# Layer 0 of a four-layer graph network: 22 strips of whole products, or seven products of half matrices

## The chip, the cores and the metric

The kernel runs on one core of a Trainium2 chip. The metric is the time on the device from the first to the last instruction, in microseconds (us). Before the change the median of three runs is 1968.97 us (1967.04 to 1970.67); the profiled execution has a span of 1967.7 us. "PE" is TensorE, "PEld" its loads of weights (the stationary operand), "DVE" VectorE, "ACT" ScalarE, "POOL" GpSimd and "SP" SyncE, whose queue starts most loads.

## The reference, cut to what matters

There are N = 2708 nodes with F = 256 features, and one weighted adjacency matrix `adj` (float32, entries of 0 or above), used by all four layers. Each layer ends with a residual and a normalisation of rows:

```python
x = layernorm(x + adj @ (x * W0))            # layer 0, W0: one factor per feature
x = layernorm(x + gat(x, adj > 0))           # layer 1: attention with 4 heads, softmax over neighbours
x = layernorm(x + signed_gat_gru(x, adj))    # layer 2: attention and two GRU cells
x = layernorm(x + linear(x, adj @ h / deg))  # layer 3: mean over neighbours
```

Layer 0 is a product of 2708x2708 by 2708x256. Layer 1 needs, for every node, `h = x @ W`, two exponentials of its attention logits (called rise and fall below), and the mask `adj > 0`.

## The kernel before, in words

The nodes are cut into NT = 22 tiles of P = 128 rows; the last has 20. `adj_t` is the matrix laid out in DRAM so that `adj_t[t]` is a strip: the 128 columns of tile t with all neighbours on the partitions, 22 blocks of 128x128 side by side.

Layer 0 (L361 to L468) goes strip by strip. For each tile t it loads a strip of 1.4 MB, and `strip_matmul` (L199) multiplies 22 blocks as weights by `x0[c]`, the 256 features of neighbour tile c as moving operand, all summed in one PSUM accumulator of 128x256. The first three strips go side by side, block after block, as x arrives (L421 to L426). The result has its rows on partitions at once. `layer0_mask` (L367) writes the 0/1 mask of the strip as fp8 for layer 1, which holds it for all nodes. `layer0_scale` (L374) multiplies by W0, `layer0_rest` adds x (L380) and normalises (`moments`, L146 to L151, where GpSimd takes a power, and L157). `layer1_projection` turns the tile (L163, two transposes), copies it out of PSUM (L165), projects it (L338, L351), takes the exponentials (L341, L342, L355) and scales `hs[t]` (L343). This is done for tile t - 1 while the products of tile t run, so only the last tile's end stands open after the last product. `xs[t]`, the normalised rows, stay in SBUF.

Layer 1 (L472 to L725) takes the nodes in pairs of groups of columns and, for each pair of heads, goes over the neighbour tiles c = 0 to 21: DVE makes two tiles p (L668) from fall, rise and mask, PE multiplies them by `hs[c]` (L650) and by columns of ones (L659).

Layers 2 and 3 (L895 on) already use a scheme of seven products. The matrix and the features are cut in two halves each way. The columns are cut in three `units` of 512, 512 and 330 columns in each half (NH = 1354); over MH = 11 pairs of neighbour tiles (c, c + 11), `step` (L977) makes four sums of blocks on DVE (L983 to L986) and seven products of 128x128 by 512 or 330 (L996), in place of eight. The features' own sums, `quarter_sums` (L961), are made once for each pair, on DVE. `sums` (L1000) puts the seven accumulators together. They fill seven of the eight PSUM banks; the eighth, `bank()` (L906), serves all other PE work, one piece at a time. Such pieces are generators, which `between()` (L1178) moves on at given places between the products. A result comes out with features on partitions, so each tile is turned back to rows by two transposes (in layer 3 at L1237).

A tile framework reorders the instructions of each engine by a planner's costs, lets each engine run its own list in order, and puts in the waits: between engines, between a load and its reader, and before a buffer is used again.

Of the kernel before, what the change touches and what calls it, by code (L numbers as in the profile page):

```python
# [27 lines left out]
def kernel(  # L28
# [83 lines left out]
    xs = [xpool.tile([P, F], F32, name=f"x{t}") for t in range(NT)]  # L112

    nc.gpsimd.memset(xs[NT - 1], 0.0)
# [13 lines left out]
    st_d = [dram.tile([2 * K, 2, W], F32, name=f"st_{u}") for u in range(len(units))]  # L128

# [146 lines left out]

    uw = const.tile([P, FC, K], F32, name="uw")
# [34 lines left out]
    if True:  # L312

        w1_a = keep.tile([P, FC, F + 2 * H], F32, name="w1_a")
        nc.scalar.dma_start(w1_a[:, :, H : H + F], w1.rearrange("(c p) j -> p c j", p=P))
# [8 lines left out]
        ps_t = ps_t_stack.enter_context(pool("ps_t", 3, space=PSUM, side="right"))  # L324
        ps_m = m_stack.enter_context(pool("ps_m", 2, space=PSUM, side="right"))
        ps_acc = acc_stack.enter_context(pool("ps_acc", 3, space=PSUM))
        if True:
# [5 lines left out]
            def layer1_projection(pool, t):  # L333
                n = sz(t)
                xt = transposed(ps_t, pool, xs[t], n, "xt")
                pm = ps_m.tile([P, 2 * F], F32, tag="pm", name="pm")
                for f in range(FC):
                    nc.tensor.matmul(  # L338
                        pm[:n, : F + H], xt[:, f, :n], w1_a[:, f, H:], start=(f == 0), stop=(f == FC - 1)
                    )  # L340
                nc.scalar.activation(rise[:n, t, :], pm[:n, F : F + H], AF.Exp, scale=1.0 - ALPHA)  # L341
                nc.scalar.activation(hs[t][:n, :, HD], pm[:n, F : F + H], AF.Exp, scale=ALPHA)  # L342
                nc.vector.tensor_tensor(  # L343
                    hs[t][:n, :, :HD],
                    pm[:n, :F].rearrange("p (h d) -> p h d", d=HD),
                    hs[t][:n, :, HD:].to_broadcast([n, H, HD]),
                    ALU.mult,
                )
                pf = ps_t.tile([P, 4, P], F32, tag="tr", name="pf")
                for f in range(FC):  # L350
                    nc.tensor.matmul(  # L351
                        pf[:, 0, :n], w1_a[:, f, :P], xt[:, f, :n], start=(f == 0), stop=(f == FC - 1)
                    )
                fall = pool.tile([H, P], F32, tag="fall", name="fall")
                nc.scalar.activation(fall[:, :n], pf[:H, 0, :n], AF.Exp, scale=ALPHA - 1.0)  # L355
                nc.gpsimd.dma_start(fall_d[:, t * P : t * P + n], fall[:, :n])

                for g in [g for g, (lo, hi) in enumerate(spans[:4]) if hi == t + 1]:
                    load_fall(falls[g // 2], g, nc.gpsimd)

            with pool("l0", 2) as l0:  # L361
                w0_b = l0.tile([P, F], F32, name="w0_b", bufs=1)
                nc.scalar.dma_start(w0_b, bcast(w0, F))

                def layer0_mask(t, s, lo=0, hi=NT):
                    n = sz(t)
                    nc.vector.tensor_scalar(  # L367
                        mask[:, lo:hi, t * P : t * P + n], s[:, lo:hi, :n], 0.0, None, ALU.is_gt, saturate=False
                    )

                def layer0_scale(t, acc):
                    n = sz(t)

                    nc.vector.tensor_tensor(xs[t][:n], acc[:n, :F], w0_b[:n], ALU.mult)  # L374

                def layer0_rest(t, acc=None):
                    n = sz(t)
                    if acc is not None:
                        layer0_scale(t, acc)
                    nc.vector.tensor_tensor(xs[t][:n], xs[t][:n], x0[t][:n], ALU.add)  # L380
                    layernorm(xs[t], xs[t], n)
                    layer1_projection(l0, t)


                ahead = 3
                with pool("prep", side="right") as prep:
                    a1_b = prep.tile([P, 2 * HD], F32, name="a1_b")
# [12 lines left out]
                    for k in range(K):  # L400
                        wk = weights(prep, f"wk{k}", gat_w[k], nc.scalar)
                        ak = prep.tile([P, F], F32, name=f"ak{k}")
# [6 lines left out]
                    strips = [l0.tile([P, NT, P], F32, tag="strip", name="strip", bufs=2) for _ in range(2)]  # L409
                    strips += [prep.tile([P, NT, P], F32, name=f"strip{t}") for t in range(2, ahead + 1)]  # L410
                    accs = [ps_acc.tile([P, 512], F32, tag="acc", name="acc") for _ in range(ahead)]
                    for c0, c1 in blocks:
                        whole = min(c1, N // P)
                        nc.sync.dma_start(
                            turn[:, c0 * F : whole * F].rearrange("p (c f) -> p c f", f=F),
                            x[c0 * P : whole * P, :].rearrange("(c p) f -> p c f", p=P),
                        )
                        for c in range(whole, c1):
                            nc.sync.dma_start(x0[c][: sz(c)], x[c * P : c * P + sz(c), :])
                        for t in range(ahead):  # L420
                            nc.sync.dma_start(strips[t][:, c0:c1], adj_t[t, :, c0:c1])  # L421
                            for c in range(c0, c1):
                                nc.tensor.matmul(  # L423
                                    accs[t][:, :F], strips[t][:, c], x0[c], start=(c == 0), stop=(c == NT - 1)
                                )
                            layer0_mask(t, strips[t], c0, c1)  # L426
                    nc.sync.dma_start(strips[ahead], adj_t[ahead])
                    for t in range(ahead):
                        layer0_scale(t, accs[t])
                    acc = ps_acc.tile([P, 512], F32, tag="acc", name="acc")  # L430
                    strip_matmul(acc[:, :F], strips[ahead], P, lambda c: x0[c])
                    for t in range(ahead):
                        layer0_rest(t)
                    nw = weights(prep, "nw", neigh_w)
                    lw = weights(prep, "lw", lin_w)
# [3 lines left out]
                    for o in range(FC):  # L439
                        pt = ps_t.tile([P, 4, P], F32, tag="tr", name="pt")  # L440
                        for i in range(FC):
                            nc.tensor.transpose(pt[:, i, :], nw[:, i, o * P : (o + 1) * P], ident)
                        nc.scalar.copy(nwt[:, o, :], pt[:, :FC, :].rearrange("p i q -> p (i q)"))
                    for i in range(FC):
                        pt = ps_m.tile([P, 2 * F], F32, tag="pm", name="pt")
                        for o in range(FC):
                            nc.tensor.matmul(
                                pt[:, :F], nwt[:, o, i * P : (i + 1) * P], lw[:, FC + o, :], start=(o == 0), stop=(o == FC - 1)
                            )
                        nc.scalar.copy(lwn2[:, i], pt[:, :F])  # L450
                    nc.gpsimd.dma_start(lwn_d[:, :, F:], lwn2)
                    layer0_mask(ahead, strips[ahead])

                keepr = mask_stack.enter_context(pool("keepr", side="right"))
                gamma_b = keepr.tile([P, F], F32, name="gamma_b")
                beta_b = keepr.tile([P, F], F32, name="beta_b")
                fallp = fall_stack.enter_context(pool("fallp", 2, side="right"))
                falls = [fallp.tile([P, H, 2 * W], F32, tag="fall_b", name="fall_b") for _ in range(2)]
                nc.sync.dma_start(gamma_b, bcast(gamma, F))
                nc.sync.dma_start(beta_b, bcast(beta, F))  # L460
                for t in range(ahead + 1, NT):
                    s = load_strip(l0, t)
                    last, acc = acc, ps_acc.tile([P, 512], F32, tag="acc", name="acc")
                    strip_matmul(acc[: sz(t), :F], s, sz(t), lambda c: x0[c])
                    layer0_mask(t, s)

                    layer0_rest(t - 1, last)
                layer0_rest(NT - 1, acc)  # L468

            m_stack.close()  # L470
            ps_u = m_stack.enter_context(pool("ps_u", space=PSUM, side="right"))
            l1 = keep_stack.enter_context(pool("l1", 2))  # L472
# [1060 lines left out]
```

## Time and profile before

| stretch of the profiled execution | us |
|---|---|
| start to the first product of layer 0 | 6.2 |
| last product of layer 0 ends | 252.5 |
| first product of layer 1 starts | 261.0 |
| end of layer 1's main loop, about | 528 |
| last product of layer 3 starts | 1940.7 |
| end | 1967.7 |

| row of the page | instructions | mean ns |
|---|---|---|
| layer 0's products, 128x256 (L199) | 836 | 379 |
| layer 0's first products (L423) | 132 | 396 |
| layers 2 and 3, products of 512 columns from p with the sums of x (L996) | 352 | 599 |
| the same of 330 columns | 176 | 443 |
| sum of blocks, 128x512 (L983) | 88 | 689 |
| sum of blocks, 128x330 (L983) | 44 | 506 |

A float32 product is two matmul instructions in the trace, so 22 x 22 products of layer 0 are 968 instructions. The mean time of a matmul runs from its start to its modelled end and overlaps the next; the distance between two starts tells what one costs in a full stream. A line of a group gives line, engine, operation, output from inputs, shapes and count, then busy us and mean ns, then the engine's idle time just before and what ended it. A line in order of time begins with start and length in us.

### The profile page before, as it was taken

Reading aid. Unit: us, or ns where it says so; the run is one execution under the profiler, and the core shown is the slowest. Engines: PE = TensorE matmul, PEld = TensorE weight load, DVE = VectorE, ACT = ScalarE, POOL = GpSimd, SP = SyncE. Lnnn points to the kernel's source line nnn. Section 1 sums busy time; section 2 is a strip of 40 time slices with the busy share of each in tenths; the row PEclk is TensorE's granted clock in tenths of the full one; section 3 lists DMA queues with packets and bytes.
Section 4 is the critical chain, followed back from the end, with each engine's and each line's share of the span. In section 5 each row is a group of like instructions: output and inputs, shape, how many; then the busy total and the mean of one; then the engine's idle time right before and its main releaser. Section 6 shows DMA issues by size and latency. Waiting matters only on the chain.

```text
span 1967.7 us, 21033 instructions
## 1 busy us (share of the span) xinstructions
PE 1895.1 (96%) x7028; PEld 945.7 (48%) x7028; DVE 1454.0 (74%) x2364; ACT 852.0 (43%) x1011; POOL 348.8 (18%) x522
## 2 busy tenths in 40 slices
PE   8999999999999999999999999999999999999995
PEld 7888822222333444445545444444445555554443
DVE  5333378898897689999987888585877758745764
ACT  0100045445603367777855656555655555211000
POOL 0211210013515302111210101020110201311211
PEclk9999999999999999999999999999999999999998
DMA  8343333432200786766475756454554535633752
GB/s 288 121 169 140 139 114 126 152 119 97 69 4 19 211 266 221 245 219 202 126 214 164 215 161 180 114 162 120 149 153 119 130 100 136 168 108 105 199 153 78
DMA packets 398210, 293.96 MB, mean 149 GB/s; under 512 B 105354, under 2 KB 379434, under 8 KB 390244
## 3 DMA queue, kind: packets, MB, share of 16 engines
q1 hardware_dynamic: 381180, 237.86, 41.2%
q0 software_dynamic: 10848, 50.23, 7.5%
q10 hardware_dynamic: 6064, 4.42, 0.7%
q8 instruction: 58, 0.95, 0.2%
q14 instruction: 60, 0.49, 0.1%
HBM read 280.03 MB, written 12.40 MB: 149 GB/s over the span
## 4 chain that ended last, share of the span: by engine, by line
PE 70%; DVE 17%; issue 5%; DMA 3%; POOL 2%; ACT 1%; SPq 1%; ACTq 0%; DVEq 0%; POOLq 0%
PE m L996 31%; PE acc L650 9%; PE acc L199 9%; DVE z L852 8%; PE bank L1056 6%; PE den L659 5%; PE bank L1032 3%; PE bank L1107 2%; DVE p L668 2%; DVE none L848 1%; POOL bn_rs L151 1%; PE acc L423 1%; PE pm L338 1%; DMA p<-in_adj_t_dram 1%; SPq L934 1%
## 5 line engine op out<-in xcount | busy, mean ns | idle before, releaser
L668 DVE SCALAR_TENSOR_TENSOR p<-fall_b,rise,mask 128x1024 f32<-128x1024 f32 (+1 forms) x264 | 298.5, 1152 | 37.1 <-PE den L659 18.6
L1198 ACT ACTIVATE p<-st,e_neg 128x1024 f32<-128x1024 f32 (+1 forms) x198 | 197.5, 1040 | 186.1 <-PE m L996 183.6
L996 PE MATMUL m<-p,xq 128*128 128x512 f32 (+1 forms) x528 | 245.6, 547 | 0.8 <-DVE p L984 0.6
L650 PE MATMUL acc<-p,h 128*64 128x512 f32 (+2 forms) x1056 | 228.4, 561 | 3.2 <-DVE p L668 2.7
L996 PE MATMUL m<-s,xq 128*128 128x512 f32 (+1 forms) x528 | 224.7, 542 | 0.4 <-DVE s L985 0.4
L852 DVE CUSTOM_DVE_ANT_0 z<-e_b,none 128x2708 f32<-128x2708 f32 (+1 forms) x66 | 196.7, 2983 | 0.3 <-DVE e_b L822 0.2
L857 ACT ACTIVATE z<-z,st 128x2708 f32<-128x2708 f32 (+1 forms) x66 | 168.5, 2553 | 64.7 <-DVE st L852 63.1
L199 PE MATMUL acc<-turn,strip 128*128 128x256 f32 (+1 forms) x836 | 187.1, 379 | 0.0
L1201 ACT ACTIVATE p<-p 128x1024 f32<-128x1024 f32 (+1 forms) x198 | 179.5, 943 | 0.3
L996 PE MATMUL m<-p,x 128*128 128x512 f32 (+1 forms) x396 | 169.5, 547 | 2.6 <-DVE p L1202 2.6
L1202 DVE TENSOR_TENSOR p<-p,blk 128x1024 f32<-128x1024 f32 (+1 forms) x132 | 142.6, 1095 | 30.9 <-ACT p L1201 16.3
L199 PEld LDWEIGHTS acc<-turn,strip 128*128 128x128 f32 (+1 forms) x836 | 151.9, 185 | 23.5 <-issue 0.2
L262 PE MATMUL s<-blk,x 128*128 128x512 f32 (+2 forms) x416 | 162.9, 545 | 0.0
L983 DVE TENSOR_TENSOR s<-p 128x512 f32<-128x512 f32 (+1 forms) x132 | 82.8, 628 | 97.9 <-PE m L996 83.8
L996 PEld LDWEIGHTS m<-p,xq 128*128 128x128 f32 x528 | 99.3, 191 | 99.6 <-issue 74.6
L996 PEld LDWEIGHTS m<-s,xq 128*128 128x128 f32 x528 | 98.7, 190 | 93.6 <-issue 70.3
L650 PEld LDWEIGHTS acc<-p,h 128*64 128x64 f32 x1056 | 65.2, 137 | 149.5 <-issue 119.8
L659 PE MATMUL den<-p,h 128*32 128x512 f32 (+2 forms) x1056 | 125.9, 557 | 2.3 <-DVE p L668 2.2
L151 POOL TENSOR_TENSOR bn_rs<-bn_rs,neg_half 128x1 f32<-128x1 f32 (+1 forms) x110 | 79.3, 722 | 242.3 <-DVE bn_rs L150 239.4
L262 PEld LDWEIGHTS s<-blk,x 128*128 128x128 f32 x416 | 77.9, 190 | 74.2 <-issue 62.5
L996 PEld LDWEIGHTS m<-p,x 128*128 128x128 f32 x396 | 74.6, 191 | 76.7 <-issue 59.1
L165 ACT COPY xt<-tr 128x256 f32<-128x256 f32 (+1 forms) x44 | 16.0, 363 | 209.2 <-PE tr L163 203.5
(228 smaller groups left out, 2587.5 us busy)
## 6 DMA issues: line engine op xcount, KB each, us to landing
blk<-in_adj_t_dram SPq DMA_DIRECT2D x172, 256.0 KB, 3.8
turn<-in_adj_dram SPq DMA_DIRECT2D x22, 1354.0 KB, 6.0
strip<-in_adj_t_dram SPq DMA_DIRECT2D x19, 1408.0 KB, 6.4
blk<-in_adj_t_dram SPq DMA_DIRECT2D x88, 192.0 KB, 3.9
turn<-in_adj_t_dram SPq DMA_DIRECT2D x65, 256.0 KB, 4.0
arow<-in_adj_dram POOLq DMA_DIRECT2D x10, 1354.0 KB, 6.7
turn<-in_adj_dram POOLq DMA_DIRECT2D x10, 1354.0 KB, 7.2
blk<-in_adj_t_dram SPq DMA_DIRECT2D x103, 128.0 KB, 2.6
```

The lines of the kernel that those rows point to most:

```text
L199: nc.tensor.matmul(acc, s[:, c, :n], rhs(c), start=(c == 0), stop=(c == NT - 1))
L262: nc.tensor.matmul(acc[f][:, :w], xs[c][:, f * P : (f + 1) * P], s[:, c - c0, :w], start=(c == 0), stop=(c == NT - 1),)
L650: nc.tensor.matmul(acc[s][i * HD : (i + 1) * HD, :ws], hs[c][:, 2 * q + i, :HD], ps[i][:, p0 : p0 + ws], **flags,)
L659: nc.tensor.matmul(den[j : j + CT, :ws], hs[c][:, 2 * q + i, HD + 1 - CT :], ps[i][:, p0 : p0 + ws], **flags,)
L668: nc.vector.scalar_tensor_tensor(p[:, :w], falls[g // 2][:, 2 * q + i, :w], rise[:, c, 2 * q + i : 2 * q + i + 1], mask[:, c, at : at + w] ...
L852: nc.vector.tensor_tensor_reduce(out=z[:n], in0=e_b[:n, k, :], in1=none[:n], scale=-1.0, scalar=HIGHEST, op0=ALU.add, op1=ALU.min, accum_o ...
L857: nc.scalar.activation(z[:n], z[:n], AF.Exp, scale=-1.0, bias=st[:n, t, 0, k : k + 1], accum_out=den[:n])
L996: nc.tensor.matmul(dst[:, :w], lt, rt, start=start, stop=stop)
L1056: nc.tensor.matmul(g[:, :w], lt, rt, start=(q == 0), stop=(q == len(terms) - 1))
L1198: nc.scalar.activation(p[:, :, :w], st_k[:, :, :w], AF.Relu, scale=-1.0, bias=e_neg[:, at, k : k + 1])
L1201: nc.scalar.activation(p[:, :, :w], p[:, :, :w], AF.Exp, scale=-1.0)
L1202: made = nc.vector.tensor_tensor(p[:, :, :w], p[:, :, :w], blk[:, i, :, :w], ALU.mult)
```

## The change

Layer 0 gets the scheme of layers 2 and 3. It goes over the three units of columns; for each of 11 pairs of neighbour tiles it loads four blocks of up to 512 columns with `load_pairs`, writes their mask (two operations), makes the four sums and the seven products. The sums of x are made on GpSimd, anew in each unit. `seven` and `combine` are `step` and `sums` of before, with the buffers handed in; `combine` copies the first accumulator straight into its output.

Results have features on partitions. So `layer0_rows` turns each tile back by transposes, scales, adds x, normalises, and stores the rows in DRAM (`x1_d`); `layer0_turned` and `layer1_projection` do what was done before. These three are pieces between products of the next unit, at three places in each step, through the one free PSUM bank. Those of the last unit come after its last product, with three banks.

The region of `xs` in SBUF serves as two of three buffers for the blocks during layer 0, so the rows are loaded back from DRAM for layer 1's end. Layer 1 goes over its neighbours in the order `by_end`, in which their tiles were finished. The small weights are loaded and prepared after the fourth step has been written down. The purpose is to do layer 0's sum with seven products of half size in place of eight.

The diff, cut to its core (`seven`, `combine`, `by_tiles`, `load_pairs` and `between` are moved up, for all layers):

```diff
-    xs = [xpool.tile([P, F], F32, name=f"x{t}") for t in range(NT)]
+    xall = xpool.tile([P, NT * F], F32, name="xall")
+    xs = [xall[:, t * F : (t + 1) * F] for t in range(NT)]
...
+    x1_d = [dram.tile([sz(t), F], F32, name=f"x1_{t}") for t in range(NT)]
...
+            def layer0_rows(t, src):
+                n = sz(t)
+                pt = bank()
+                for f in range(FC):
+                    nc.tensor.transpose(pt[:n, f * P : (f + 1) * P], src[:, f, :n], ident)
+                r = l0.tile([P, F], F32, tag="row", name="row", bufs=3)
+                nc.vector.tensor_tensor(r[:n], pt[:n, :F], w0_b[:n], ALU.mult)
+                nc.vector.tensor_tensor(r[:n], r[:n], x0[t][:n], ALU.add)
+                layernorm(r, r, n)
+                nc.gpsimd.dma_start(x1_d[t], r[:n])
+                return t, r
...
+                for i in range(len(tiles) + 2):
+                    if i < len(tiles):
+                        got.append(layer0_rows(*tiles[i]))
+                        yield
+                    if i >= 2:
+                        layer1_projection(*turned[i - 2])
+                        yield
+                    if 0 < i <= len(tiles):
+                        turned.append(layer0_turned(*got[i - 1]))
+                        yield
...
-                for t in range(ahead + 1, NT):
-                    s = load_strip(l0, t)
-                    last, acc = acc, ps_acc.tile([P, 512], F32, tag="acc", name="acc")
-                    strip_matmul(acc[: sz(t), :F], s, sz(t), lambda c: x0[c])
-                    layer0_mask(t, s)
-                    layer0_rest(t - 1, last)
-                layer0_rest(NT - 1, acc)
+                for u, (a, w) in enumerate(units):
+                    m = accumulators(ps_a)
+                    for c in range(MH):
+                        if u == 0:
+                            for t in (c, c + MH):
+                                nc.sync.dma_start(x0[t][: sz(t)], x[t * P : t * P + sz(t), :])
+                        i = (u * MH + c) % 3
+                        if i < 2:
+                            pa = xall[:, i * 4 * W : (i + 1) * 4 * W].rearrange("p (m h w) -> p m h w", m=2, h=2)
+                        else:
+                            pa = l0.tile([P, 2, 2, W], F32, tag="p", name="p")
+                        load_pairs(u, c, pa)
+                        for j in range(2):
+                            nc.vector.tensor_scalar(
+                                mask[:, c + j * MH].rearrange("p (h n) -> p h n", h=2)[:, :, a : a + w],
+                                pa[:, j, :, :w], 0.0, None, ALU.is_gt, saturate=False,
+                            )
+                        s = l0.tile([P, 3, W], F32, tag="s", name="s", bufs=2)
+                        tt = l0.tile([P, 4, P], F32, tag="xq", name="xq", bufs=3)
+                        seven(
+                            m, pa, s, x0, quarter_sums(nc.gpsimd, tt, x0, c), c, w, c == 0, c == MH - 1, (1, 3, 5)
+                        )
+                        if u == 0 and c == 3:
+                            small_weights()
+                            later.append(neigh_weights())
+                    y = l0.tile([P, FC, 2, W], F32, tag="y", name="y")
+                    combine(m, w, y)
...
+                    later.append(rows0(u, y))
+                ps0_stack.close()
+                banks = ps_t = ps_t_stack.enter_context(pool("ps_t", 3, space=PSUM, side="right"))
+                while later:
+                    between()
...
+            for t in by_end:
+                nc.sync.dma_start(xs[t][: sz(t)], x1_d[t])
...
-                        for c in range(NT):
+                        for j, c in enumerate(by_end):
```

## The prediction

> **What bounds the kernel now.** I read the page's busy shares and the chain that ended last, then layer 0 and layer 3 in tables of windows, because layer 3 already runs the seven products that layer 0 is to get.
>
> ```profile
> PE 1895.1 (96%) x7028; PEld 945.7 (48%) x7028; DVE 1454.0 (74%) x2364; ACT 852.0 (43%) x1011; POOL 348.8 (18%) x522
> PE 70%; DVE 17%; issue 5%; DMA 3%; POOL 2%; ACT 1%; SPq 1%; ACTq 0%; DVEq 0%; POOLq 0%
> ```
>
> TensorE is busy 96% of the span and makes up 70% of the chain. So work taken off it is worth its time, if nothing else becomes the bound.
>
> ```profile
> 0.00:50.00 50.00, 42.19 (x187) 36.58 (x188) 25.39 (x68) 1.66 (x2) 4.79 (x18) 1.00 0.84 285
> 40.00:252.00 212.00, 212.00 (x1041) 182.74 (x1040) 80.37 (x156) 23.66 (x86) 42.40 (x68) 1.00 0.40 144
> 1824.00:1892.00 68.00, 67.55 (x168) 30.13 (x167) 41.77 (x84) 0.58 (x1) 12.37 (x20) 1.00 0.67 185
> 1892.00:1941.00 49.00, 46.52 (x171) 29.80 (x169) 33.47 (x88) 0.43 (x1) 8.17 (x14) 1.00 0.56 146
> ```
>
> The columns after the length are PE, PEld, DVE, ACT, POOL (busy us and count), clock, DMA share, GB/s. Layer 0 (second line) has PE full and DVE only 38% busy. Layer 3's second unit of columns (third line) keeps PE full too, with DVE at 61%; its narrow third unit (fourth line) already loses 2.5 us of PE with DVE at 68%. That is the first warning.
>
> ```profile
> L996 PE MATMUL m<-p,xq 128*128 128x512 f32 x352 | 182.1, 599 | 0.6 <-DVE p L984 0.4
> L199 PE MATMUL acc<-turn,strip 128*128 128x256 f32 x792 | 177.2, 379 | 0.0
> L983 DVE TENSOR_TENSOR s<-p 128x512 f32<-128x512 f32 x88 | 60.6, 689 | 82.7 <-PE m L996 74.3 <-DMA p<-in_adj_t_dram 8.3
> L367 DVE TENSOR_SCALAR mask<-strip 128x2816 fp8e4<-128x2816 f32 x18 | 29.3, 1627 | 47.7 <-DMA strip<-in_adj_t_dram 47.7
> ```
>
> The means of matmuls overlap, so I take their pitch from starts in the order of time: 40 of 128x256 in 8.81 us, 0.216 us each; two steps' starts in layer 3 are 6.01 us apart at 512 columns (14 matmuls, 0.429 each) and 3.886 at 330.
>
> ```profile
> 252.57 0.41 DVE L374 TENSOR_TENSOR x<-acc,w_b 20x256 f32<-20x256 f32 x1 [1.85 <-PE acc L199]
> 258.10 0.41 DVE L343 TENSOR_TENSOR h<-pm,h 20x256 f32<-20x256 f32 x1 [1.82 <-ACT h L342]
> 260.96 1.97 PE L650 MATMUL acc<-p,h 128*64 128x512 f32 x4 [2.65 <-DVE p L668]
> 241.58 0.82 DVE L380 TENSOR_TENSOR x<-x,turn 128x256 f32<-128x256 f32 x1
> 241.40 0.72 POOL L535 TENSOR_TENSOR x<-x,beta_b 128x256 f32<-128x256 f32 x1 [7.75 <-PE tr L163]
> 1430.99 2.34 POOL L953 TENSOR_TENSOR blk<-blk,offdiag 128x128 f32<-128x128 f32 x1 [10.46 <-DMA blk<-in_adj_t_dram]
> 1433.65 0.41 POOL L953 TENSOR_TENSOR blk<-blk,offdiag 128x128 f32<-128x128 f32 x1 [0.31 <-DMA blk<-in_adj_t_dram]
> ```
>
> Layer 0's last product ends at 252.5 and layer 1's first starts at 260.96: one row tile's end lies between, 8.5 us. The last four lines show GpSimd and VectorE in each other's way: a 256-wide sum that takes 0.41 us at the least took 0.82 beside a GpSimd operation, and a GpSimd operation of 0.41 took 2.34 while VectorE ran sums back to back.
>
> [...]
>
> **The change, part by part.**
> *Products.* Removed: 968 matmuls (132 at L423, 836 at L199) x 0.216 = 209 us. Added: 22 steps of 512 columns x 6.01 = 132.2 and 11 of 330 x 3.886 = 42.7, together 174.9. PE gains 34 us. Turning rows back adds two transposes a tile, 0.22 us a pair in layer 3, x 22 = 4.8. Net 29 us less PE: this is what can be won.
>
> *Start.* Now PE starts at 6.23 and by 50 us has lost 7.8. In the built order VectorE does seven small weight operations ahead of the first mask; the first of these starts at 8.23 now (it waits for a load), so masks begin near 11 and PE's third product near 14.5, with two done (1.7 us). PE also waits for a transpose of a weight whose load is tenth on its queue. Loss 12.8, so +5. Unit 0 then ends at 14.5 + 75 products x 0.858 + 2 for weights = 81.
>
> *VectorE and GpSimd beside the products.* A step of 512 needs two masks of 1024 (from 1.63 us for 2816 and 0.43 for 512: 0.70 each) and four sums of 0.69: 4.2 us; of 330: 1.0 + 4 x 0.50 = 3.0. A row tile needs 0.42 + 0.41 + 0.42 + 0.17 + 0.15 + 0.41 + 0.42 = 2.4 us and a wait for GpSimd's power of some 0.75. GpSimd gets four quarter sums a step, 0.41 each alone: 1.7 us, and a tile's power (0.56) and two DMA issues (0.6 each). Two bounds on their meeting: no cost, [...]. For a wide step with a tile the second gives 5.0 (masks, sums, two row operations) + 3.4 = 8.4 us against PE's 6.0 + 1.9 (transposes 0.44, projection 1.5); for a narrow one 3.8 + 3.4 = 7.2 against 5.8. Unit 1 has 7 tiles, unit 2 has 8 (in about 8 of its steps). Unit 1: 7 x 8.4 + 4 x 6.0 = 83, against PE 66 + 14 = 80. Unit 2: 8 x 7.2 + 3 x 4.7 = 72, against PE 42.7 + 15.5 = 58. All small PE work goes through one PSUM bank, so each waits for the reader of the one before; late readers hold up PE. I take 82 and 74 (2 us for loads queued behind a reload, see next); ends 79 and 60, or 88 and 82.
>
> *Tail.* The last unit leaves seven tiles after its last product, where now it is one. Combining takes 2.4 us (layer 3's end: 1941.3 to 1943.7), the first transposes 0.4. A tile costs VectorE 2.4 us of pitch with the power's wait filled, so 17; the last turn and projection 2.5, then 2.5 to the first product of layer 1: 25. The built order of GpSimd has sums of reloaded rows with beta among the powers: store issue 0.58, landing 2.8 (median of like stores), reload issue 0.5 and landing 2.6, the sum 0.72. That round trip of 7.2 us is shorter than two or three tiles, but the powers of tiles 18 and 20 stand behind such sums and VectorE waits behind the powers: some 2.6 us each, twice. I take 30.5 (25 to 36), against 8.5 now.
>
> *Order of layer 1's neighbours, combining without a copy of its own, x reloaded:* nothing; the same operations in another order, under PE's products of layer 1 (261.8 of 266 us busy). More DMA: 22 reloads of 128 KB, hidden there.
>
> Sum to layer 1's first product: 81 + 82 + 74 + 30.5 = 267.5, now 261. Forecast: +6.5, 1968.97 + 6.5 = 1975.5, say 1976.
>
> **The rivals.**
> *PE stays the bound* (as in layer 3 at 1824 to 1892): units end at 79, 79 and 60 us each, tail 25: 243 to 247, so -14: 1955. For it: VectorE's order is planned, and layer 3 lost only 0.45 us in its wide unit. Against: layer 3 has no masks, no quarter sums on GpSimd after its first unit, fewer row operations, and its narrow unit lost 2.5 us all the same.
> *A draw:* contention costs half, unit 2 takes 68 and the tail 28: 81 + 82 + 68 + 28 = 259, 1967. For it: GpSimd may slip into VectorE's gaps. Against: unit 2 has nearly none.
> *VectorE and GpSimd take turns badly:* units 1 and 2 at 88 and 82, tail 36: 287, 1995. For it: powers of 1.46 us occur in the trace where 0.56 is usual. Against: wide steps have slack.
> *DMA bound in unit 0:* 11.5 MB of matrix, 2.8 of x and some 1.5 of weights at the 288 GB/s that the first slice shows take 55 us, under the 66 of products; 4% at most.
>
> **How the numbers follow.** Forecast 0.48, PE-bound rival 0.24, draw 0.14, bad turns 0.10, DMA 0.04. The range, 1958 to 1992, leaves out the best of the PE-bound cases and the worst of the contention. Faster by over 0.2% (under 1965): the PE-bound cases and a few draws, 0.27. Within: 0.15. Slower: 0.58.
>
> **What would show it.** Right: layer 1's first product near 267; VectorE above 85% busy in unit 2, PE idle behind VectorE's reads of the bank and behind mask and sums; quarter sums of GpSimd well over 0.41 us on the mean; some 28 us and more of nearly idle PE before layer 1. Wrong: PE above 97% in units 1 and 2 (then it is faster), or layer 1 itself longer or shorter by more than 3 us, which no step here foresees.

## The result, and the profile after

The changed kernel takes 1989.94 us (median of four, 1987.03 to 1993.66) against 1969.12 for the kernel before: a ratio of 1.0107, 95% interval 1.0088 to 1.0127. It is slower, as forecast, and by 21 us instead of 7. The measured time lies inside the forecast range.

The page of the changed kernel, busy shares and chain by engine:

```profile
PE 1877.6 (95%) x6566; PEld 859.8 (43%) x6566; DVE 1552.4 (78%) x2537; ACT 850.5 (43%) x1014; POOL 440.0 (22%) x682
PE 61%; DVE 16%; DMA 9%; issue 5%; ACT 4%; POOL 4%; SPq 1%; ACTq 0%; DVEq 0%; POOLq 0%
```

TensorE has 17 us less to do, and its share of the chain fell from 70% to 61%: the products did get cheaper, and other things took their place. Where, a table of windows shows, cut at the ends of the three units and at layer 1's first product (after the length: PE, PEld, DVE, ACT, POOL busy and count, granted clock, DMA share, GB/s):

```profile
0.00:25.00 25.00, 8.90 (x12) 3.60 (x13) 10.75 (x21) 1.66 (x2) 7.88 (x24) 0.81 0.80 219
25.00:89.70 64.70, 64.54 (x156) 29.08 (x156) 52.84 (x80) 1.70 (x4) 34.05 (x46) 1.00 0.83 231
89.70:176.50 86.80, 80.96 (x240) 39.18 (x239) 64.38 (x119) 5.80 (x29) 39.61 (x70) 1.00 0.52 143
176.50:246.00 69.50, 61.34 (x250) 41.16 (x249) 53.58 (x121) 8.84 (x34) 40.85 (x73) 0.98 0.53 143
246.00:279.00 33.00, 18.18 (x89) 12.97 (x87) 21.89 (x57) 9.92 (x32) 20.23 (x36) 0.83 0.28 92
```

Unit 2's last product ends at 246.6 us. Layer 1's first product starts at 278.98 where it started at 260.96. From there to the end it is 1706.2 us, before 1706.7: the whole loss lies in layer 0. Up to layer 1's first product TensorE is busy 233.9 us (before 248.6) and idle 45.1 (before 12.4). Of the idle time 16 us lie in the first 25 us, 14 in units 1 and 2, and 15 in the tail; between 25 and 90 us there is next to none (0.2).

In the start TensorE makes two products from 8.7 us on. Then it waits for the load of a weight that it transposes, and after that for a load of the matrix (waits of the first 26 us):

```profile
PE bank L550 <- DMA nw<-in_L_gnn_neigh_W_dram: 3.8, 1, 3.8
PE m L348 <- DMA xall<-in_adj_t_dram: 3.5, 1, 3.5
```

The third product starts at 20.3 us, and the granted clock is 0.50 until 25.5.

What holds TensorE up in units 1 and 2 (waiting operation, what it waited for, total us, times, longest):

```profile
PE bank L454 <- DVE h L473: 7.3, 7, 3.3
PE bank L464 <- DVE row L444: 2.9, 4, 1.1
PE m L348 <- POOL xq L322: 1.2, 1, 1.2
```

`bank` is the one free PSUM bank: each transpose or projection waits until the reader of the piece before, which stands in VectorE's list, has run. The products themselves hardly wait for VectorE's sums. The longest of these waits, 3.3 us, ended at 225.9 us. From 226.9 to 230.3 the granted clock was 0.50, and four matmuls of L464 took 1.94 us there (1.14 at 104.8 us, at a clock of 1.00); so this long wait was followed by slow matmuls too.

The end of the tail, in order of time:

```profile
275.92 0.18 ACT L472 ACTIVATE fall<-bank 4x20 f32<-4x20 f32 x1 [1.80 <-DMA fall_d<-fall]
276.12 0.41 DVE L473 TENSOR_TENSOR h<-bank,h 20x256 f32<-20x256 f32 x1 [3.61 <-ACT fall L472]
...
276.46 4.85 DVE L816 SCALAR_TENSOR_TENSOR p<-fall_b,rise,mask 128x1024 f32<-128x1024 f32 x4
...
278.98 2.83 PE L798 MATMUL acc<-p,h 128*64 128x512 f32 x6 [5.12 <-DVE p L816]
```

The exponential for `fall` of the last, small tile waits for the store of an earlier one (there are two buffers), VectorE's scaling of h waits for it, and everything else behind that.

### The profile page after: what moved, and what is told of

It is laid out like the page before. It is cut to its first block, busy times and chain, and to the rows that moved or that the text cites. A ratio compares the mean times of both kernels' runs of the same rounds, so it can differ in the third digit from the quotient of the medians.

```text
span 1985.2 us, 20983 instructions
## 1 busy us (share of the span) xinstructions
PE 1877.6 (95%) x6566; PEld 859.8 (43%) x6566; DVE 1552.4 (78%) x2537; ACT 850.5 (43%) x1014; POOL 440.0 (22%) x682
## 4 chain that ended last, share of the span: by engine, by line
PE 61%; DVE 16%; DMA 9%; issue 5%; ACT 4%; POOL 4%; SPq 1%; ACTq 0%; DVEq 0%; POOLq 0%
PE m L348 37%; PE bank L1130 6%; DVE z L1000 6%; PE acc L798 5%; DMA turn<-in_adj_dram 5%; PE bank L1106 3%; PE den L807 3%; PE s L263 2%; ACT turn L745 2%; PE bank L1181 2%; POOL bn_rs L152 2%; ACT turn L747 2%; DVE p L816 1%; DVE none L996 1%; DMA xall<-in_adj_t_dram 1%
## 5 line engine op out<-in xcount | busy, mean ns | idle before, releaser
L348 PE MATMUL m<-s,xq 128*128 128x512 f32 (+1 forms) x660 | 282.2, 543 | 0.4 <-DVE s L337 0.4
L348 PE MATMUL m<-p,xq 128*128 128x512 f32 (+1 forms) x572 | 265.6, 547 | 1.3 <-DVE p L336 0.6
L348 PEld LDWEIGHTS m<-s,xq 128*128 128x128 f32 x660 | 123.0, 191 | 114.1 <-issue 86.2
L348 PE MATMUL m<-p,xall 128*128 128x512 f32 (+1 forms) x396 | 169.7, 547 | 2.5 <-DVE p L1249 2.5
L263 PE MATMUL s<-blk,xall 128*128 128x512 f32 (+2 forms) x416 | 164.2, 549 | 0.0
L263 PEld LDWEIGHTS s<-blk,xall 128*128 128x128 f32 x416 | 78.7, 192 | 74.8 <-issue 63.2
L1078 POOL TENSOR_TENSOR blk<-blk,offdiag 128x128 f32<-128x128 f32 (+3 forms) x50 | 43.1, 861 | 299.2 <-DMA blk<-in_adj_t_dram 264.2
L348 PEld LDWEIGHTS m<-p,xall 128*128 128x128 f32 x396 | 74.8, 191 | 76.5 <-issue 59.5
L745 ACT ACTIVATE turn<-turn 128x2708 f32<-128x2708 f32 (+1 forms) x22 | 54.2, 2462 | 98.4 <-DMA turn<-in_adj_dram 97.7
L338 DVE TENSOR_TENSOR s<-p,s 128x512 f32<-128x512 f32 (+1 forms) x143 | 91.0, 636 | 2.1
```

The lines of the kernel that those rows point to most:

```text
L263: nc.tensor.matmul(acc[f][:, :w], xs[c][:, f * P : (f + 1) * P], s[:, c - c0, :w], start=(c == 0), stop=(c == NT - 1),)
L348: nc.tensor.matmul(dst[:, :w], lt, rt, start=start, stop=stop)
```

## The experiments

My theory after the traces was that the loss is made of the start, the hand-over of the one bank, and the tail. The rivals were that GpSimd's sums of x slow VectorE's operations beside them, that the DMA bounds the first unit, and that VectorE's load as such is the limit. Each run was timed in five rounds beside the kernel before on the same chip.

The table has the ratio to the kernel before, and from the profile the time at which ScalarE starts to copy the first accumulator of each unit (a mark 2 to 5 us ahead of the unit's end), the start of layer 1's first and the end of its last product. With * layer 1 starts ahead of the last tiles. Layer 1's loop is counted to its last product, 643.6 us in the kernel before; at about 528 us only two of its three pairs of groups of columns are done. What a unit "took" or is longer or shorter by is, below, the time from mark to mark. The kernel before took 1969.12, 1970.95, 1973.02 and 1972.25 us beside the changed kernel, e1 to e4, e5 to e8 and e9 to e11, so runs of different groups are compared by the ratio and not by their medians. By the ratio only e2, e7, e8, e10 and e11 are clear of the changed kernel's interval.

| kernel | ratio (95%) | unit 0 | unit 1 | unit 2 | first | last |
|---|---|---|---|---|---|---|
| before | 1 | | | | 261.0 | 643.6 |
| after | 1.0107 (1.0088 to 1.0127) | 84.7 | 171.6 | 243.3 | 279.0 | 661.3 |
| e1 fall buffers | 1.0090 (1.0076 to 1.0104) | 83.5 | 170.5 | 242.7 | 273.9 | 662.4 |
| e2 bank by ScalarE | 1.0056 (1.0041 to 1.0071) | 84.5 | 165.3 | 230.7 | 266.4 | 655.5 |
| e3 weights late | 1.0095 (1.0072 to 1.0117) | 82.2 | 168.2 | 239.9 | 274.1 | 662.9 |
| e4 layer 1 ahead | 1.0068 (1.0046 to 1.0090) | 84.3 | 171.3 | 243.3 | 250.2* | 657.2 |
| e5 beta in layer 0 | 1.0086 (1.0062 to 1.0109) | 82.3 | 171.9 | 243.4 | 276.4 | 667.1 |
| e6 weights in unit 1 | 1.0072 (1.0050 to 1.0095) | 71.3 | 165.7 | 237.9 | 273.1 | 662.1 |
| e7 x sums on VectorE | 1.0053 (1.0034 to 1.0072) | 83.8 | 168.2 | 235.9 | 271.4 | 656.8 |
| e8 all together | 0.9987 (0.9972 to 1.0002) | 72.3 | 160.8 | 230.4 | 240.8* | 644.0 |
| e9 masks on ScalarE | 1.0089 (1.0070 to 1.0108) | 81.2 | 163.0 | 238.3 | 273.5 | 660.7 |
| e10 all, x sums on VectorE | 0.9965 (0.9955 to 0.9975) | 71.0 | 156.8 | 225.9 | 235.2* | 638.4 |
| e11 as e10, masks on ScalarE | 0.9967 (0.9952 to 0.9983) | 72.2 | 160.8 | 231.3 | 238.2* | 642.0 |

### e1: more buffers for fall

```diff
-                fall = l0.tile([H, P], F32, tag="fall", name="fall", bufs=2)
+                fall = l0.tile([H, P], F32, tag="fall", name="fall", bufs=8)
```

> The changed kernel with eight buffers for fall in layer 0 instead of two. In its trace the last tile's exponential for fall waits 1.8 us for the store of an earlier fall, and VectorE's scaling of h then waits 3.6 us. If this wait is a part of the tail's length, layer 1's first product comes 2 to 3.5 us earlier and the kernel takes 1987 (1986 to 1988). If the tail is set by the pitch of VectorE's row work alone, nothing moves (within 1 us).

From the mark of unit 2 to layer 1's first product it is 31.2 us instead of 35.6. The wait is gone, and so are, by the planner's choice, the sums with beta among the tail's powers, so that the 4.4 us are not the wait's alone; VectorE's idle time at the wait was 3.6 us. But the time came out at 1988.71, within the noise of the changed kernel. The gain was given back in layer 1, whose loop took 388.5 us instead of 382.3. The groups of VectorE's tiles p and of GpSimd's sums with beta in this kernel, 284 to 314 us (last: busy us, mean ns, idle before):

```profile
L816 DVE SCALAR_TENSOR_TENSOR p<-fall_b,rise,mask 128x1024 f32<-128x1024 f32 x20 | 32.6, 1700 | 0.0
L683 POOL TENSOR_TENSOR xall<-xall,beta_b 128x256 f32<-128x256 f32 x16 | 26.8, 1711 | 0.0
```

The same stretch of the changed kernel (289 to 319 us), where these sums had mostly run in the tail and the end of unit 2:

```profile
L816 DVE SCALAR_TENSOR_TENSOR p<-fall_b,rise,mask 128x1024 f32<-128x1024 f32 x22 | 27.4, 1281 | 3.1 <-PE den L807 1.8 <-PE acc L798 1.2
```

The planner had put the 22 sums elsewhere, and there each tile p took a third longer. TensorE was busy 26.3 of those 30 us.

### e2: the bank emptied by ScalarE

```diff
+                nc.scalar.copy(r[:n], pt[:n, :F])
-                nc.vector.tensor_tensor(r[:n], pt[:n, :F], w0_b[:n], ALU.mult)
+                nc.vector.tensor_tensor(r[:n], r[:n], w0_b[:n], ALU.mult)
...
+                hp = l0.tile([P, 4 * P], F32, tag="hp", name="hp", bufs=2)
+                nc.scalar.copy(hp[:n, : F + H], pm[:n])
+                nc.scalar.copy(hp[:H, 3 * P : 3 * P + n], pf[:H, :n])
+                pm, pf = hp[:, : F + H], hp[:, 3 * P :]
```

> The changed kernel, with the one free PSUM bank emptied by ScalarE copies (rows, and the projection with its logits) in place of VectorE's reads and the exponentials; VectorE then reads SBUF. Theory: TensorE's idle time in units 1 and 2 (14 us in the two) is mostly the wait for late readers of that bank, which stand in VectorE's full list; ScalarE is under 10% busy there, so about 8 us come back: 1982 (1979 to 1985), units 1 and 2 at about 82 and 66 us. Rival, [...]: no change in the units' lengths, or slightly longer [...]: 1990 (1988 to 1993).

The kernel took 1981.25 us. Unit 1 took 80.8 us (86.9 before the edit) and unit 2 65.4 (71.8). That is the expected size, and the "no change" of the rival, GpSimd's sums of x as the cause, is out. (Unit 2's granted clock is 1.00 here and was 0.98, which by estimate, 2% of 71.8 us, is worth some 1.5 us.) TensorE's waits in the two units:

```profile
PE bank L455 <- DVE bn_mv L149: 3.2, 2, 1.7
PE bank L455 <- DVE row L158: 2.3, 2, 1.8
```

The waits for readers of the bank are gone; what is left are transposes that wait for the normalised row itself. Layer 1's loop again took 389.2 us, with the sums with beta in its first 40 us: 6.9 us of the 12.6 won were given back.

### e3 and e6: when the weights come

```diff
-                        if u == 0 and c == 3:
+                        if u == 0 and c == 4:
...
+                        nc.scalar.copy(wk[:, 0, :1], s[:, 0, :1])
                         nc.scalar.dma_start(wk, gat_w[k].rearrange("(c p) j -> p c j", p=P))
```

Each weight's buffer gets such a write from a sum of that step first, so that its load can't come earlier.

> The changed kernel, with the loads of the small weights of layers 1 to 3 (and their work on VectorE and TensorE) held back until the fifth step of layer 0's first unit has made its first sum. Theory: the first unit ended 8.7 us later than forecast because masks and sums stand behind small weight work that waits for loads on a crowded set of queues; without it the first unit ends 5 to 8 us earlier and the kernel takes 1984 (1981 to 1987). Rival, that the matrix's own loads bound the start (219 GB/s in the first 25 us): the first unit ends at most 2 us earlier: 1989 (1987 to 1991).

> The changed kernel with layer 1's small weights held back to the seventh step of the first unit, and those of layers 2 and 3 to the third step of the second, where the DMA share is 0.52 and not 0.9. With all of them held back to the fifth step of the first unit the start was full from 12 us on, but then VectorE stood in front of weights that were late at a DMA share of 0.97 to 0.99, and TensorE idle for 6 us. Theory: the small loads and the matrix together are more than the DMA engines can bring in that unit, and without them the unit ends 6 to 8 us earlier than in the changed kernel (accumulator copied at 77 to 79 us instead of 84.7): 1984 (1981 to 1987). Rival: the matrix and x alone bound the first unit, which ends at 82 or later: 1989 (1987 to 1991).

In e3 (all weights at step 5) the first unit won 2.5 us only, and the time, 1990.04 us, is the rival's. Windows of e3:

```profile
0.00:25.00 25.00, 18.30 (x33) 7.58 (x34) 16.34 (x23) 1.28 (x1) 15.89 (x34) 1.00 0.91 255
25.00:46.00 21.00, 21.00 (x50) 9.12 (x48) 16.86 (x34) 1.51 (x12) 7.81 (x12) 1.00 0.87 227
46.00:55.00 9.00, 3.79 (x8) 1.56 (x8) 6.61 (x10) 0.28 (x2) 3.37 (x5) 0.84 0.94 278
```

The start was as wanted (18.3 us busy in 25 instead of 8.9), then the weights' loads came at a DMA share of 0.94, VectorE stood before a weight that was not there, and the sums of the next step behind it. In e6 layer 1's weights come at step 7 of the first unit (`c == 6`), the others at step 3 of the second:

```profile
0.00:25.00 25.00, 17.43 (x35) 7.01 (x36) 15.98 (x23) 1.28 (x1) 13.93 (x33) 1.00 0.88 248
25.00:73.80 48.80, 48.80 (x115) 21.58 (x114) 41.04 (x60) 0.87 (x3) 24.43 (x35) 1.00 0.79 221
```

From 25 us on TensorE has no gap, and the mark comes 13.4 us earlier, at 71.3. So matrix and x alone do not bound the unit from there on, as the rival had it; matrix, x and weights in the same 60 us, with VectorE's list held at each late weight, do. Unit 1 then carries the weights and takes 94.4 us instead of 86.9, so 5.9 us are left at its end. The forecast of the unit's end was beaten, that of the time missed: the kernel took 1988.49 us (1.0072). Layer 1's loop took 389.0 us; 4.3 of that is one wait of TensorE for ScalarE's copy of a finished accumulator, 1.1 in the changed kernel. e5 (6.3 us) and e3 (4.1) have the same wait.

### e4: layer 1 ahead of the tail

```diff
-                while later:
-                    between()
...
                             for part in (heads, totals)[:: 1 if j % 2 == 0 else -1]:
                                 part(c, ps, dict(start=(j == 0), stop=(j == NT - 1)))
+                            if g == 0 and q == 0:
+                                for _ in range(2):
+                                    between()
```

> The changed kernel, with layer 1's first round over neighbours begun before the last unit's seven tiles are finished: their pieces stand between the products of the fifteen neighbours that are done, with the tail's buffers in the region of x that is free by then, so that no pool has to be closed first. Theory: the tail of 32.5 us, in which TensorE is busy 18 us, some of it at a low clock, is the largest term of the loss, and 10 to 18 us of it come back: 1975 (1972 to 1980). Rival: VectorE, 88% busy in layer 1, has no room for the tail's 22 us, and becomes the bound of that first round: 1987 (1984 to 1992).

This kernel took 1986.06 us. It leaves out the degrees of two row tiles, a little work of layer 1, so its time is if anything too good. From the mark of unit 2 to layer 1's last product it is 414.0 us instead of 418.0: 4 us, not 10 to 18. Layer 1's first product starts at 250.2, but then TensorE waits 6.8 us for tiles p and 2.7 for rows up to 360 us, with VectorE 89% busy from 250 to 290. The sums with beta stand in the same stretch again (1.06 us each, tiles p at 1.37). The rival was nearer.

### e5: beta added in layer 0

```diff
+                rb = l0.tile([P, F], F32, tag="rb", name="rb", bufs=2)
+                nc.gpsimd.tensor_tensor(rb[:n], r[:n], beta_b[:n], ALU.add)
-                nc.gpsimd.dma_start(x1_d[t], r[:n])
+                nc.gpsimd.dma_start(x1_d[t], rb[:n])
...
-                    nc.gpsimd.tensor_tensor(xs[t][:n], xs[t][:n], beta_b[:n], ALU.add)
```

> The kernel with eight fall buffers, and in addition beta added on GpSimd to each row tile before it is stored (so in layer 0's units and tail), in place of the 22 sums with beta on GpSimd after the rows have been loaded back. With eight buffers alone layer 1 began 5 us earlier, but GpSimd's 22 sums stood back to back in layer 1's first 40 us (1.7 us each), VectorE's tiles p took 1.75 us instead of 1.28, and TensorE was busy 8.8 us in 10. Theory: that is what gave the gain back, and with the sums moved into layer 0, where VectorE has about a fifth of its time free, layer 1's first 40 us are full again: 1984 (1981 to 1986.5). Rival: the sums cost the same wherever they stand, and units 1 and 2 get longer by 4 to 5 us: 1988 (1986.5 to 1990).

The kernel took 1989.03 us (1.0086, e1 1.0090): no gain. The mechanism was right, the sum was not. TensorE's 30 us in layer 1 are full (30.00 busy, 26.31 in e1), and its first 352 matmul records there took 62.7 us, not 69.4. But unit 1 and the tail were 2.6 and 1.8 us longer than in e1, and the wait for ScalarE's copy (6.3 us) came on top.

### e7 and e9: VectorE's load, or its turns with GpSimd

```diff
-                            m, pa, s, x0, quarter_sums(nc.gpsimd, tt, x0, c), c, w, c == 0, c == MH - 1, (1, 3, 5)
+                            m, pa, s, x0, quarter_sums(nc.vector, tt, x0, c), c, w, c == 0, c == MH - 1, (1, 3, 5)
```

> The changed kernel with the sums of x (four of 128x128 a step) on VectorE instead of GpSimd. Theory: [...] VectorE then has 1 us more to do in each of 33 steps and reads the bank later: slower by 2 to 10 us, 1995. Rival: [...] then the masks and sums get back to 0.69 us and the powers to 0.56, and units 1 and 2 together get shorter by more than 4 us: 1984.

The kernel took 1982.85 us. My theory, that late readers of the bank hold up units 1 and 2 and GpSimd's sums of x do not, had the wrong sign; the rival, that these sums do, had the right one. Units 1 and 2 got 2.5 and 4.1 us shorter (some 1.5 us of it by the clock in unit 2, an estimate as in e2). Masks and sums went back to 0.69 us, as the rival said; GpSimd's powers did not (0.705 us, before 0.627). The two units of e7, up to the end of their products:

```profile
86.20:170.60 84.40, 80.22 (x240) 39.31 (x239) 68.80 (x165) 5.80 (x29) 15.63 (x24) 1.00 0.53 149
170.60:238.20 67.60, 62.58 (x255) 40.47 (x254) 55.46 (x158) 8.74 (x34) 25.56 (x39) 1.00 0.58 154
```

VectorE, layer 0 in the changed kernel (25 to 246 us):

```profile
L335 DVE TENSOR_TENSOR s<-xall 128x512 f32<-128x512 f32 x14 | 10.8, 770 | 8.3 <-PE m L348 8.1
...
L445 DVE TENSOR_TENSOR row<-row,turn 128x256 f32<-128x256 f32 x15 | 8.7, 577 | 0.1
L158 DVE TENSOR_SCALAR row<-row,bn_mv,bn_rs 128x256 f32<-128x256 f32 x15 | 7.7, 512 | 7.3 <-POOL bn_rs L152 7.3
```

and in e7 (25 to 240 us), with one of the four sums of x:

```profile
L335 DVE TENSOR_TENSOR s<-xall 128x512 f32<-128x512 f32 x14 | 9.6, 686 | 0.2 <-PE m L348 0.2
L319 DVE TENSOR_TENSOR xq<-turn 128x128 f32<-128x128 f32 x31 | 8.8, 284 | 4.2 <-PE m L348 4.2
L445 DVE TENSOR_TENSOR row<-row,turn 128x256 f32<-128x256 f32 x15 | 6.2, 416 | 0.0
L158 DVE TENSOR_SCALAR row<-row,bn_mv,bn_rs 128x256 f32<-128x256 f32 x15 | 6.2, 413 | 7.1 <-POOL bn_rs L152 7.0
```

A sum of x takes VectorE 0.28 us, GpSimd 0.54 to 0.73. In the two windows VectorE was given 81 sums of x, 23.3 us, and was busy only 6.3 us more (124.3 for 118.0): GpSimd's "free" help had cost it some 17 us. (The expectation of e10 has 119.7 for 124.3, from windows that did not reach to the units' ends.)

For e9 the mask is written by `nc.scalar.activation(..., AF.Sign)` instead of `nc.vector.tensor_scalar(..., ALU.is_gt)`, the same for a matrix without negative entries, as this one is.

> The changed kernel with layer 0's masks written by ScalarE as the sign of an entry (the same for a matrix without negative entries, as this one is) instead of VectorE. It takes 1.0 to 1.4 us a step from VectorE, some 40 us in the three units, and nothing else. If VectorE's load (its own work and its turns with GpSimd) is what makes readers late in units 1 and 2, these get shorter by 6 to 12 us together and the kernel takes 1981 (1977 to 1985). If the single bank is held up by latency alone (semaphores, the order of reads), they get shorter by less than 3 us: 1988 (1986 to 1991).

The kernel took 1989.73 us (1.0089), no gain clear of the noise. Its units 1 and 2:

```profile
83.60:165.40 81.80, 79.05 (x238) 39.24 (x237) 51.06 (x97) 26.56 (x51) 39.25 (x68) 1.00 0.54 151
165.40:240.60 75.20, 65.81 (x254) 44.17 (x253) 43.08 (x101) 22.21 (x54) 42.02 (x74) 0.93 0.52 138
```

VectorE is busy 94.1 us in the two instead of 118.0, and they are 1.5 us shorter together: unit 1 by 5.0, while unit 2 is 3.5 longer. But the edit did more than take work off VectorE. The exponentials stand behind ScalarE's masks now, so that VectorE waited 15.2 us for them (8.3 in the changed kernel), and TensorE waited 3.4 us in unit 2 for a copy by ScalarE. TensorE also ran 9.5 us of unit 2 at half clock, 3.4 in the changed kernel, which by estimate, half of the 6.1 us more, makes 3 us. So a fifth less work on VectorE did not shorten the units while the bank's readers came no earlier; what it would bring with readers as prompt as before is not shown. With e2 it speaks for the reader: what counted was how soon the bank was read.

### e8, e10, e11: together

> All that has helped, together: the bank emptied by ScalarE, the weights held back as in the run with them in unit 1, the seven last tiles worked off between layer 1's first products, beta added before the rows are stored, more buffers for fall in the tail. Theory, by the parts: 1990 - 9 (bank) - 6 (weights) - 10 (tail inside layer 1 with no beta sums there) = 1965 (1958 to 1970), about 5 us under the kernel before. Rival: layer 1, where VectorE is 88 to 92% busy, gives most of it back: 1975 (1970 to 1980), slower than before.

> All that helped, and the sums of x on VectorE too. Moving them alone shortened units 1 and 2 by 6.6 us, with VectorE as busy as before in the two (119.7 for 118.0 us) though it had 4 sums more in each step: [...] Theory: the same gain here, 1971 - 6 = 1965 (1961 to 1969), under the kernel before. Rival: with the bank emptied by ScalarE the products are no longer held up, and nothing is gained: 1971 (1969 to 1974).

> As the run with all that helped and the sums of x on VectorE, and masks of layer 0 on ScalarE. Theory: VectorE falls to some 65% busy in the three units and these come to TensorE's own 66, 82 and 60 us and a start of 8: 1960 (1956 to 1966). Rival: first the mask and then the sum that overwrites the block is a longer way at the start of each step with two engines in turn, and TensorE waits there: 1968 (1964 to 1975).

e8 joins the edits of e2 (in the units, not in the tail), e6, e4 (with all degrees) and e5; fall has six buffers in the tail. It took 1970.71 us, 0.9987 of the kernel before, which is not clear of no change: between theory and rival, just inside the rival's range. e10 adds the edit of e7 and took 1964.61 us, as its theory had it: the best here, 0.35% under the kernel before (0.25 to 0.45). Its windows, by unit:

```profile
0.00:73.50 73.50, 65.73 (x149) 29.12 (x150) 57.88 (x135) 2.15 (x4) 2.01 (x13) 1.00 0.84 234
73.50:159.30 85.80, 81.83 (x252) 41.38 (x251) 75.63 (x178) 15.38 (x66) 25.80 (x33) 1.00 0.64 175
159.30:228.00 68.70, 61.21 (x247) 41.10 (x245) 54.80 (x155) 16.25 (x58) 25.04 (x37) 0.98 0.52 142
```

GpSimd is nearly idle in the first unit, and its beta sums stand in the others. Layer 1's last product ends at 638.4 us: 5.2 us ahead of the kernel before. e11, with masks on ScalarE as well, gains nothing more (1965.16 us, inside the ranges of its theory and of its rival, and its marks come 1 to 5 us later than e10's).

## Why the prediction was right in sign, and short by 14 us

- *Products, net 29 us less PE.* Half of it shows: 14.7 us less busy up to layer 1. The busy time beside the products, taken at their pitch (209 and 174.9 us), is 59.0 us instead of 39.6, where I had added 4.8 for transposes. The prediction gave a low clock no price, though before the change the granted clock was 0.71 from 260 to 270 us. Up to layer 1's first product TensorE was busy 13.8 us at half clock here (5.9 in the start, 3.4 in unit 2, 4.5 in the tail), before the change next to nothing. By estimate, half of the 13.8, that is some 7 us; the rest is not separated.
- *Start, unit 0 ends at 81.* This step failed in size: 89.7. That is 8.7 of the 11.5 us by which layer 1's first product was late against the forecast. The mechanism was named rightly (masks behind weights, TensorE behind the transpose of a weight), but I counted one early delay and took the loads after it to flow. The third product started at 20.3 us and not at 14.5, which is 5.8 us; the half clock up to 25.5 is another 2.6 by estimate. e3 and e6 show that the small loads hold up VectorE where they meet the matrix: with most of them held back to the next unit the mark comes 13.4 us earlier. The DMA rival had the right resource and the wrong sum: the total, 55 us by its estimate, would fit in, but not all of it at the times at which it was asked for.
- *VectorE and GpSimd beside the products, 82 and 74.* Measured 86.8 and 70 (to the end of unit 2's last product): 156.8 for 156. That the sum fits so well is luck: unit 1 was 4.8 us over and unit 2 4 us under. Quarter sums of 0.54 to 0.73 us were as said. Two reasons were not: VectorE is 77% busy in unit 2 and not over 85%, and a fifth less of its work did not shorten the units (e9). What I had as a half-sentence, small work through one bank, is what TensorE waits for (e2), and GpSimd's sums of x slow VectorE's operations around its readers (e7: without them the two units are 6.6 us shorter). The forecast's dearer bound, 5.0 + 3.4 us in a wide step, puts VectorE's masks, sums and two row operations and GpSimd's work one after the other; that was my estimate. In the trace the row operation that reads PSUM (L444) took 0.413 us beside GpSimd's sums and 0.416 once they had left GpSimd (e7). The one after it with both inputs in SBUF (L445) went from 0.577 to 0.416, the tensor_scalar of L158 from 0.512 to 0.413, the wide mask (L578, from xall) from 0.756 to 0.691.
- *Tail, 30.5.* Measured 32.5. Two powers do stand behind sums with beta, at 264.4 and 268.0 us, but VectorE waits 0.4 and 1.0 us for them and not 2.6 each. In their place stood the wait for a fall buffer, in which VectorE idles 3.6 us and which I had missed: two buffers, and a store still under way when the last, small tile comes.
- *Order of layer 1's neighbours, combining, reload: nothing.* Right for this kernel (1706.2 and 1706.7 us to the end), but the reload carries GpSimd's 22 sums with it. Where they fall is up to the planner: 13 of them here from 240.1 to 249.9 us, at the end of unit 2; all in layer 1 in e1, where TensorE lost 3.7 us in 30.

Of the signs announced, the reads of the bank and the longer quarter sums came. Layer 1's first product near 267 (279.0) did not, nor did the nearly idle stretch ahead of it: TensorE is busy 18.2 of the tail's 33 us. The bad-turns rival (1995) was nearest in time, but for another reason: units 1 and 2 together took no longer than in my forecast.

What stays open is layer 1: its loop takes 382 to 383 us before and after, and 385 to 391 in e1 to e3, e5 to e7 and e9. Sums with beta (e1, e2) and the wait for ScalarE's copy (e3, e5, e6) explain most of it, in e7 and e9 only a part.

## What to carry to other kernels

When work is moved from a full engine to others, price the places where results change hands: here an idle ScalarE that copied out the one PSUM bank at once gave 12.6 us back by layer 1, while taking a fifth of VectorE's work away, with the readers no earlier, gave 1.5 us in the two units. Help from GpSimd was not free here while VectorE ran sums (of 23.3 us taken off VectorE some 17 came back): do the small sums on VectorE and compare. And look for what is given back after the stage that was mended, since a planner puts freed work somewhere else.

## What the runs showed of the hardware

In e1, GpSimd and VectorE, each with operations on SBUF back to back, kept in step, one of each every 1.7 us: tiles p went from 1.28 to 1.70 us and GpSimd's sum of 128x256 from 0.72 (at 261.4 us in the changed kernel) to 1.71. Both lost, though 1.7 is less than the sum of the two, 2.0. In the changed kernel one sum of VectorE (L445 at 105.3 us, both inputs in SBUF) took 1.80 us instead of 0.41, while GpSimd ran three sums of x in a row. With sums of 128x128 (0.28 us on VectorE, 0.54 to 0.73 on GpSimd) most of the help was eaten up: of 23.3 us that GpSimd took off VectorE, some 17 came back as slower operations, and without that help the kernel was faster (e7: ratio 1.0053 against 1.0107).
